# Gate and up in two passes: first units and handover to down reordered, bias table made once per group

## The chip, the cores and the metric

The kernel runs on one core of one Trainium2 chip, as one launch. The metric is the device time of that core in microseconds. Of each kernel the median of several runs is taken; one further execution is recorded by the hardware profiler, and the profile and the trace come from it.

## The reference

x has 1024 rows of 512. It is normalised (layernorm); the result goes through a quantised gated feed-forward block, whose output passes a silu and gates the output of an ALiBi attention with 32 query heads in 8 groups of 4. Weights of the feed-forward block are integers with a zero and a scale per 128 input rows.

```python
def dequantize(w, s, z):                      # groups of 128 rows
    return (w - repeat(z, 128)) * repeat(s, 128)

xn   = (x - mean(x)) / sqrt(var(x) + 1e-5)
gate = silu(xn @ dequantize(gate_w, gate_s, gate_z))     # 512 -> 1792
up   = xn @ dequantize(up_w, up_s, up_z)
ffn  = (gate * up) @ dequantize(down_w, down_s, down_z)  # 1792 -> 512

q, k, v = xn @ Wq.T, xn @ Wk.T, xn @ Wv.T     # 32, 8, 8 heads of 128
q, k    = rmsnorm(q, q_norm_w), rmsnorm(k, k_norm_w)
bias    = where(rel > 0, -1e30, slope[head] * rel)       # rel = key - query
attn    = softmax(q @ k.T / sqrt(128) + bias) @ v        # per head
out     = x + (attn @ Wo.T) * silu(ffn)
```

## The kernel before

**Order.** Every engine's instructions stand in the order in which the program text issues them: the schedule is manual on all five engines, there is no planner. All DMAs are issued on SP's queue. So a line's place in the text decides what it waits behind on its engine. Matmuls of float data run as two or three products of high and low parts; `split_r` (L95) makes such a pair with an ACT copy (L97, the high part) and a DVE subtraction (L99, the low part).

**Layernorm and the first units.** There are 8 row tiles of 128; tiles 0 to 3 are the first half of the columns of xnT, tiles 4 to 7 the second. A tile gets statistics (L281) and moments (L284) on DVE, is normalised (L302 on DVE for the first half, L300 on ACT for the second), transposed by TensorE (L309) and split into xth and xtl. PSUM in this stage is four buffers of two banks each (`pair`, L139), handed out in the order in which they are released.

Gate and up are 14 units of 128 hidden columns. A unit's weights are loaded as integers (`gu_load`, L154), its zeros are spread over the partitions by two matmuls into z_ps (`gu_spread`, L163), and DVE subtracts them (`gu_subtract`, L174, the tile guq). The scales are applied to the four partial sums j = 0 to 3 of the input groups: j even by ACT (L189), j odd by DVE, which adds the scaled sum to the one before (L191); POOL adds the two results (`gu_total`, L195). m = 0 is gate, m = 1 is up. ACT's silu (L199) and DVE's product h (L204) follow one unit later (`gu_finish`, with `behind` holding the unit that is still to be finished). Units 0, 1 and 2 are done twice with half the columns, since the second half of xnT isn't there yet: (0,0), (1,0), (2,0), then (0,1), (1,1), (2,1). Units 3 to 13 take all 1024 columns. The second half's statistics stand inside and after unit (0,0), tiles 4 and 5 are normalised before unit (1,0) and tiles 6 and 7 after it.

**Down.** 14 passes, one for each 128 hidden rows, two column halves each, with twelve 128x512 matmuls to a half (L103 to L105), summed in PSUM over all passes. `dn_load` loads integers, zeros and scales (two passes ahead), `dn_dequant` subtracts on DVE (L389) and multiplies on POOL (L390) one pass ahead, `dn_split_w` and `dn_split_h` make the parts. Pass 0's weights are dequantised before unit 13 and split halfway in it; pass 1's within pass 0. Ahead of down stand also the first value projection's column norms (`norms`, L456 and the seed L82, L83), their application (`scale`, L463) and the norm weights (`norm_weights`, L411 to L417).

**Projections and attention.** Twelve projections (kv, q, q, four times) make q, k and v, which go to scratch memory and back. q's and k's inverse norms are refined on POOL in three newton steps (`newton`, L520 to L523). Attention runs over 8 groups, four blocks of 256 queries and four heads: scores on PE, then DVE adds the bias table `trel` times a scalar and takes the row minimum (L718), ACT takes the exponential (L719) and the high half-precision part (L729), DVE the low part (L738), SP transposes by DMA to pT (L739), PE multiplies with the values and with Wo. The table is made for each head and block by POOL (`relative`, L695), one unit ahead; its width is that of the block.

Of the kernel before, what the change touches and what calls it, by code (L numbers as in the profile page):

```python
# [21 lines left out]
P = 128  # L22
S = 1024
# [39 lines left out]


@with_exitstack
def attention_gated_by_ffn_kernel(ctx, tc, x, gu_w, gu_z, gu_s, dn_w, dn_z, dn_s, wq, wkv, wo, qnw, knw, out):
# [47 lines left out]
    cs = const.tile([P, 1], F32, name="cs")  # L114
# [61 lines left out]
    gu_sums, behind = {}, []  # L176

    def gu_scaled(unit, m, j, ps):
# [3 lines left out]
        if j == 0:  # L182
            two = wp.tile([P, 2, S], F32, tag=("wh", "wl")[m], name=f"g{m}_{it}_{tb}", bufs=2)
            for i in range(2):
                gu_sums[unit, m, 2 * i] = two[:, i, :w]
# [4 lines left out]
        else:  # L190
            ve.scalar_tensor_tensor(a, ps, scale, a, ALU.mult, ALU.add)  # L191

# [13 lines left out]
    def gu_finish(k):  # L206

        if behind:
            (gu_gate, gu_h)[k](behind[0])

    def gu_unit(it, tb, subtract=None, first=False, halfway=lambda: None, late=False):
        unit = (it, tb)
        w = gu_int[it]
        if subtract is not None:
            gu_spread(subtract)
        if not late:
            gu_finish(0)
        for m in range(2):
            ws = slice(m * P, m * P + P)
            banks = {}  # L220
            for j in range(KT):
# [30 lines left out]
                elif j % 2 and not (first and m == 0):  # L252
                    for i in (j - 1, j):
                        gu_scaled(unit, m, i, banks[i])
                elif j == KT - 1:
                    for i in range(KT):
                        gu_scaled(unit, m, i, banks[i])
                if m == 0 and j == 1 and not late:
                    gu_finish(1)
            gu_total(unit, m)  # L260
            if m == 0:
                halfway()
        if late:
            gu_finish(0)
            gu_finish(1)
        behind[:] = [unit]
# [25 lines left out]
    def ln_norm(t):  # L292
        half, r = divmod(t, HT)
        xn[t] = gp.tile([P, DM], F32, tag="hl" if t % 2 else "hh", name=f"xn{t}", bufs=3)
        if half:
            if r == 0:
# [7 lines left out]
    def ln_transpose(t):  # L304
        if t % 2 == 0:
            xt_ps["pair"] = pair(f"xt_ps{t}")
        xt_ps[t] = xt_ps["pair"][:, t % 2, :].rearrange("p (j c) -> p j c", j=KT)
# [34 lines left out]
    gu_load(3)  # L342

    def second_stats(*ts):
        for t in ts:
            ln_stats(t)
        for t in ts:
            ln_moments(t)

    def second_split(*ts):  # L350
        for t in ts:
            ln_transpose(t)
        for t in ts:
            ln_split(t)

    gu_unit(0, 0, 1, True, halfway=lambda: second_stats(4, 5))
    second_stats(6, 7)
    ln_rstd(1)
    ln_norm(4)
    ln_norm(5)  # L360
    gu_unit(1, 0, 2, late=True)
    ln_norm(6)
    ln_norm(7)
    second_split(4, 5)
    gu_unit(2, 0, halfway=lambda: second_split(6, 7))
    gu_unit(0, 1)
    gu_unit(1, 1)
    gu_unit(2, 1, 3)
# [4 lines left out]
    def dn_load(it):  # L373
        if it % 2 == 0:
            wi = gp.tile([P, 2, DM], I32, tag="wi", name=f"dni{it}", bufs=3)
            sp.dma_start(wi, dn_w[it * P : (it + 2) * P, :].rearrange("(t p) c -> p t c", p=P))
            wf = wi.bitcast(F32)
# [571 lines left out]
```

## Time and profile before

| | |
|---|---|
| median of 3 runs | 1113.13 us (1112.53 to 1117.06) |
| the profiled execution | 1118.34 us |
| its span | 1116.6 us |
| mean granted clock of TensorE | 0.989 |
| DVE busy | 877.4 us (79%) |
| ACT busy | 763.5 us (68%) |
| POOL busy | 507.5 us (45%) |
| bias table L695 on POOL | 128 operations, 145.9 us |
| unit 3's first matmul | 54.22 us |
| first down matmul; second pass | 148.32 us; 159.47 us |

Times in the profile are counted from the start of the span. A group of instructions is named by its line, engine, operation, output and inputs; "xcount" is how many there are. A wait is put down to the instruction that released it. The granted clock is the share of full speed at which TensorE may run[...]. PE is TensorE, PEld its weight loads.

### The profile page before, as it was taken

What the parts mean: (1) busy time and instruction counts of PE and PEld (TensorE: products, weight loads), DVE (VectorE), ACT (ScalarE), POOL (GpSimd) and SP (SyncE); (2) the same over time, 40 slices, a digit from 0 to 9 for tenths busy, and PEclk for the clock granted to TensorE, in tenths of its full rate; (3) what the DMA queues carried; (4) which work ended last, traced back from release to release, by engine and by line L of the source; (5) the groups of instructions that cost most, each with busy time, mean ns of one, the idle gap of its engine ahead of it and who ended that gap; (6) DMA issues with size and microseconds to landing.
All of it is one profiled execution on the core that took longest, in us unless ns stands there. A gap on an engine that the chain in (4) does not pass through costs nothing.

```text
span 1116.6 us, 18808 instructions
## 1 busy us (share of the span) xinstructions
PE 1048.9 (94%) x5900; PEld 765.6 (69%) x5900; DVE 877.4 (79%) x1698; ACT 763.5 (68%) x2031; POOL 507.5 (45%) x617
## 2 busy tenths in 40 slices
PE   7899979999999999897899999999999999998996
PEld 5677658878888888675566666666666676665664
DVE  6788984525687677688779898798897988968985
ACT  4766543456657575477779688796896888867872
POOL 1455552215676677562324435245243342424642
PEclk9899999999999999999999999999999999999999
DMA  5133225344998989969999999999999999998994
GB/s 176 45 102 102 76 79 155 88 137 113 223 225 170 248 188 232 253 153 215 221 170 210 177 215 215 185 210 197 197 207 183 193 223 177 195 213 188 230 191 122
DMA packets 461634, 198.13 MB, mean 177 GB/s; under 512 B 395810, under 2 KB 421726, under 8 KB 461534
## 3 DMA queue, kind: packets, MB, share of 16 engines
q1 hardware_dynamic: 461534, 196.93, 81.2%
q8 instruction: 46, 0.75, 0.3%
q14 instruction: 54, 0.44, 0.1%
HBM read 71.03 MB, written 29.36 MB: 90 GB/s over the span
## 4 chain that ended last, share of the span: by engine, by line
PE 55%; DMA 14%; DVE 13%; ACT 9%; issue 6%; POOL 3%; SPq 1%; DVEq 0%; ACTq 0%; POOLq 0%
DMA pT<-p 12%; PE gu_ps L226 5%; PE ps_q L103 4%; PE ps_q L104 4%; PE ps_q L105 4%; PE s L103 3%; PE av L103 3%; PE s L104 3%; PE s L105 3%; PE av L104 3%; PE av L105 3%; ACT p L729 3%; PE op L103 3%; PE op L105 3%; PE op L104 2%
## 5 line engine op out<-in xcount | busy, mean ns | idle before, releaser
L695 POOL TENSOR_SCALAR trel<-nrel,rc 128x1024 f32<-128x1024 f32 (+3 forms) x128 | 145.9, 1140 | 304.8 <-DVE row L718 303.0
L738 DVE SCALAR_TENSOR_TENSOR p<-pf,row,p 128x1024 f16<-128x1024 f32 (+7 forms) x256 | 226.0, 883 | 73.4 <-ACT p L729 71.3
L729 ACT ACTIVATE p<-pf,row 128x1024 f16<-128x1024 f32 (+7 forms) x256 | 197.1, 770 | 71.1 <-DMA pT<-p 67.7
L719 ACT ACTIVATE pf<-pf,row 128x1024 f32<-128x1024 f32 (+7 forms) x256 | 197.2, 770 | 50.7 <-DVE row L718 48.5
L718 DVE CUSTOM_DVE_ANT_0 pf<-s,trel,cs 128x1024 f32<-128x1024 f32 (+7 forms) x256 | 207.0, 809 | 2.5 <-PE s L105 1.3
L103 PE MATMUL av<-pT,vT 128*128 128x256 f16 (+1 forms) x640 | 170.8, 267 | 22.3 <-DMA pT<-p 21.8
L104 PE MATMUL av<-pT,vT 128*128 128x256 f16 (+1 forms) x640 | 168.1, 263 | 0.0
L105 PE MATMUL av<-pT,vT 128*128 128x256 f16 (+1 forms) x640 | 167.9, 263 | 0.0
L103 PE MATMUL s<-kT,qT 128*128 128x512 f16 (+3 forms) x384 | 125.2, 326 | 14.1 <-DVE row L718 13.4
L103 PEld LDWEIGHTS <-vT 128*128 128x128 f16 x640 | 62.3, 97 | 101.3 <-issue 81.1
L104 PE MATMUL s<-kT,qT 128*128 128x512 f16 (+3 forms) x384 | 125.2, 326 | 0.0
L105 PE MATMUL s<-kT,qT 128*128 128x512 f16 (+3 forms) x384 | 123.6, 326 | 0.0
L103 PE MATMUL op<-woh,oh 128*128 128x512 f32 x248 | 121.4, 489 | 0.0
L103 PE MATMUL ps_q<-wh_q,xth 128*128 128x512 f32 x256 | 101.3, 396 | 0.0
L105 PE MATMUL ps_q<-wh_q,xtl 128*128 128x512 f32 x256 | 99.7, 390 | 0.0
L104 PE MATMUL ps_q<-wl_q,xth 128*128 128x512 f32 x256 | 99.6, 389 | 0.0
L105 PE MATMUL op<-woh,ol 128*128 128x512 f32 x248 | 98.1, 396 | 0.0
L104 PE MATMUL op<-wol,oh 128*128 128x512 f32 x248 | 97.7, 394 | 0.3 <-POOL wol L689 0.3
L689 POOL TENSOR_TENSOR wol<-wor,woh 128x512 fp32r<-128x512 f32 x32 | 55.4, 1730 | 46.5 <-ACT woh L688 46.5
L195 POOL TENSOR_TENSOR g_None<-g_None 128x1024 f32<-128x1024 f32 x22 | 54.7, 2486 | 43.1 <-DVE g_None L191 43.0
L104 PEld LDWEIGHTS <-vT 128*128 128x128 f16 x640 | 63.2, 99 | 13.7 <-issue 4.3
L529 POOL TENSOR_TENSOR f_q<-f_q,inv_q 128x512 f32<-128x512 f32 x64 | 71.4, 1134 | 1.4
(155 smaller groups left out, 2427.7 us busy)
## 6 DMA issues: line engine op xcount, KB each, us to landing
qd<-tr_q SPq DMA_DIRECT2D x64, 256.0 KB, 3.4
qT<-qd SPq DMA_DIRECT2D x32, 512.0 KB, 4.2
wq<-in_wq SPq DMA_DIRECT2D x32, 256.0 KB, 3.9
wor<-in_wo SPq DMA_DIRECT2D x32, 256.0 KB, 3.3
gui<-in_gu_w SPq DMA_DIRECT2D x13, 512.0 KB, 3.6
wkv<-in_wkv SPq DMA_DIRECT2D x16, 256.0 KB, 3.9
vd<-v SPq DMA_DIRECT2D x64, 64.0 KB, 2.8
kd<-tr_kv SPq DMA_DIRECT2D x64, 64.0 KB, 1.9
```

The costliest lines, as they stand in the source:

```text
L103: te.matmul(ps, lhsT=lh, rhs=rh, start=first, stop=False)
L104: te.matmul(ps, lhsT=lh, rhs=rl, start=False, stop=False)
L105: te.matmul(ps, lhsT=ll, rhs=rh, start=False, stop=last)
L195: ge.tensor_tensor(a, a, gu_sums.pop((unit, m, 2)), ALU.add)
L226: te.matmul(banks[j][:, k, :], lhsT=w[:, j, ws], rhs=x[:, j, k * 512 : k * 512 + 512], start=x is xth, stop=x is xtl)
L529: ge.tensor_tensor(f, f, ib, ALU.mult)
L689: ge.tensor_tensor(wol[g, i], raw, woh[g, i].bitcast(F32), ALU.subtract)
L695: ge.tensor_scalar(trel[u][:, S - w :], nrel[:, S - w :], rc, float(SLOPES[g * NH + hh]), ALU.mult, ALU.mult)
L718: ve.tensor_tensor_reduce(p, ps, trel[u][:, S - w :], cs, 3e38, ALU.add, ALU.min, least[:, c])
L719: se.activation(p, p, AF.Exp, bias=least[:, c], scale=-1.0, accum_out=total[:, c])
L729: se.activation(p16[u, qt][:, :, 0, :], pf[u, qt], AF.Copy, scale=scale[:, qt : qt + 1])
L738: ve.scalar_tensor_tensor(lo, p, scale, hi, ALU.mult, ALU.subtract)
```

## The change

It has three parts.

1. First units. Each transposed tile gets a PSUM pair of its own. The zero subtraction of units 1 and 2 and the loads of units 3 to 5 stand ahead of unit (0,0). The second half's statistics, moments, inverse deviation and norms all stand after unit (0,0); tiles 6 and 7 are normalised on DVE instead of ACT. All four tiles are transposed and split after unit (1,0). Unit (0,0) is evicted by `gu_first`: ACT scales three of the four sums, and the fourth, on DVE, with two additions on POOL, is held back (`rest`) until the norms have been issued. The silu and the product h of two-pass units stand at the ends of later units.
2. Handover. The value norms of the first projection are made one unit later, their application in down pass 9, the norm weights in pass 5. Pass 0's weights are dequantised in unit 12 and pass 1's in unit 13, with both operations on DVE; pass 0's parts are made in the first quarter of unit 13. Unit 13's totals, silu and h move to passes 1 to 4. In down, loads run three passes ahead, dequantisation two, and both h halves are split one pass ahead.
3. Bias table. One table for each group, for the last of its four slopes, over all 1024 columns. Each head's scalar in L718 is a column of `cs`, which holds the ratio of its slope to the last one's; q is scaled by the inverse ratio in the last newton step, which takes four small operations in place of one.

```diff
+STEEPER = [float(SLOPES[i]) / float(SLOPES[NH - 1]) for i in range(NH)]
...
-    cs = const.tile([P, 1], F32, name="cs")
+    cs = const.tile([P, NH], F32, name="cs")
...
-    gu_sums, behind = {}, []
+    gu_sums, behind = {}, ([], [])
...
-            two = wp.tile([P, 2, S], F32, tag=("wh", "wl")[m], name=f"g{m}_{it}_{tb}", bufs=2)
+            if tb is None or m == 0:
+                tag = m if tb is None else (it + tb + 1) % 2
+                two = gu_sums[unit, "tile"] = wp.tile([P, 2, S], F32, tag=("wh", "wl")[tag], name=f"g{m}_{it}_{tb}", bufs=2)
+            else:
+                two = gu_sums[unit, "tile"][:, :, 512:]
...
+    def gu_first(m, banks):
+
+        two = wp.tile([P, 2, S], F32, tag=("wh", "wl")[m], name=f"g{m}_first", bufs=2)
+        parts = [two[:, 0, :512], two[:, 1, :512], two[:, 0, 512:]]
+        for j, a in enumerate(parts):
+            se.activation(a, banks[j], AF.Copy, scale=gsT[:, 0, m, j : j + 1])
+        gu_sums[(0, 0), m, 0] = parts[0]
+
+        def rest():
+            a, b, c = parts
+            ve.scalar_tensor_tensor(c, banks[3], gsT[:, 0, m, 3:4], c, ALU.mult, ALU.add)
+            ge.tensor_tensor(a, a, b, ALU.add)
+            ge.tensor_tensor(a, a, c, ALU.add)
+
+        return rest
...
-        if behind:
-            (gu_gate, gu_h)[k](behind[0])
-
-    def gu_unit(it, tb, subtract=None, first=False, halfway=lambda: None, late=False):
+        if behind[k]:
+            (gu_gate, gu_h)[k](behind[k].pop(0))
+
+    def gu_unit(it, tb, subtract=None, first=False, halfway=lambda: None, finish=True, meanwhile=lambda: None, total=True):
         unit = (it, tb)
         w = gu_int[it]
+        rest = []
         if subtract is not None:
             gu_spread(subtract)
-        if not late:
+        if finish and tb is None:
...
-                elif j % 2 and not (first and m == 0):
+                elif j % 2 and not first:
                     for i in (j - 1, j):
                         gu_scaled(unit, m, i, banks[i])
-                elif j == KT - 1:
-                    for i in range(KT):
-                        gu_scaled(unit, m, i, banks[i])
-                if m == 0 and j == 1 and not late:
+                if m == 0 and j == 1 and finish and tb is None:
                     gu_finish(1)
-            gu_total(unit, m)
+                    meanwhile()
+            if first:
+                rest.append(gu_first(m, banks))
+            elif total:
+                gu_total(unit, m)
+            for _ in range(finish if tb is not None else 0):
+                gu_finish(m)
             if m == 0:
                 halfway()
-        if late:
-            gu_finish(0)
-            gu_finish(1)
-        behind[:] = [unit]
+        for k in range(2):
+            behind[k].append(unit)
+        return rest
...
-        if half:
-            if r == 0:
+        if t in (HT, HT + 1):
+            if t == HT:
...
-        if t % 2 == 0:
-            xt_ps["pair"] = pair(f"xt_ps{t}")
-        xt_ps[t] = xt_ps["pair"][:, t % 2, :].rearrange("p (j c) -> p j c", j=KT)
+        xt_ps[t] = pair(f"xt_ps{t}")[:, 0, :].rearrange("p (j c) -> p j c", j=KT)
...
-    gu_load(3)
-
-    def second_stats(*ts):
-        for t in ts:
-            ln_stats(t)
-        for t in ts:
-            ln_moments(t)
-
-    def second_split(*ts):
-        for t in ts:
-            ln_transpose(t)
-        for t in ts:
-            ln_split(t)
-
-    gu_unit(0, 0, 1, True, halfway=lambda: second_stats(4, 5))
-    second_stats(6, 7)
+    for it in (1, 2):
+        gu_spread(it)
+        gu_subtract(it)
+    for it in (3, 4, 5):
+        gu_load(it)
+
+    rest = gu_unit(0, 0, first=True, finish=False)
+    for t in range(HT, NT):
+        ln_stats(t)
+        if t > HT:
+            ln_moments(t - 1)
+    ln_moments(NT - 1)
     ln_rstd(1)
-    ln_norm(4)
-    ln_norm(5)
-    gu_unit(1, 0, 2, late=True)
-    ln_norm(6)
-    ln_norm(7)
-    second_split(4, 5)
-    gu_unit(2, 0, halfway=lambda: second_split(6, 7))
-    gu_unit(0, 1)
-    gu_unit(1, 1)
-    gu_unit(2, 1, 3)
+    for t in range(HT, NT):
+        ln_norm(t)
+    for f in rest:
+        f()
+    gu_unit(1, 0, finish=False)
+    for t in range(HT, NT):
+        ln_transpose(t)
+        ln_split(t)
+    gu_unit(2, 0, finish=2)
+    gu_unit(0, 1, finish=1)
+    gu_unit(1, 1, finish=1)
+    gu_unit(2, 1, 3, finish=1)
...
-            wf = wi.bitcast(F32)
-            wh = gp.tile([P, 2, DM], F32R, tag="wq", name=f"dnh{it}", bufs=3)
-            wl = gp.tile([P, 2, DM], F32R, tag="dwl", name=f"dnl{it}")
-            dn_raw["pair"] = (wi, wf, wh, wl)
+            dn_raw["pair"] = (wi, wi.bitcast(F32))
...
-    def dn_dequant(it):
-        wi, wf, wh, wl, zi, si = dn_raw[it]
+    def dn_dequant(it, engine=ge):
+        wi, wf, zi, si = dn_raw[it]
         ve.tensor_tensor(wf, wi, zi, ALU.subtract)
-        ge.tensor_tensor(wf, wf, si, ALU.mult)
+        engine.tensor_tensor(wf, wf, si, ALU.mult)
     def dn_split_w(it):
-        wi, wf, wh, wl, zi, si = dn_raw.pop(it)
-        split_r(wf, wh, wl)
-        dn_w_hl[it] = (wh, wl)
+        if it % 2 == 0:
+            wh = gp.tile([P, 2, DM], F32R, tag="wq", name=f"dnh{it}", bufs=3)
+            wl = gp.tile([P, 2, DM], F32R, tag="dwl", name=f"dnl{it}")
+            dn_w_hl["pair"] = (wh, wl)
+        dn_w_hl[it] = tuple(w[:, it % 2, :] for w in dn_w_hl["pair"])
+        split_r(dn_raw.pop(it)[1], *dn_w_hl[it])
...
-        ve.tensor_scalar(cs, wm, 1.0 / (Q_SCALE * Q_SCALE * math.sqrt(HD)), None, ALU.mult)
-        ve.reciprocal(rc, cs)
+        for i in range(NH):
+            ve.tensor_scalar(cs[:, i : i + 1], wm, STEEPER[i] / (Q_SCALE * Q_SCALE * math.sqrt(HD)), None, ALU.mult)
+        ve.reciprocal(rc, cs[:, NH - 1 : NH])
...
-            c = Q_SCALE if last and self.kind == "q" else 1.0
             ge.tensor_tensor(w, a, y, ALU.mult)
             ge.tensor_tensor(w, w, y, ALU.mult)
-            ge.tensor_scalar(w, w, -0.5 * c, 1.5 * c, ALU.mult, ALU.add)
+            if last and self.kind == "q":
+                for i in range(NH):
+                    c = Q_SCALE / STEEPER[i]
+                    wi = w.rearrange("p (t g) -> p g t", g=NH)[:, i]
+                    ge.tensor_scalar(wi, wi, -0.5 * c, 1.5 * c, ALU.mult, ALU.add)
+            else:
+                ge.tensor_scalar(w, w, -0.5, 1.5, ALU.mult, ALU.add)
...
-    def down_first():
+    def down_begin():
         dn_split_w(0)
         dn_split_h(0, 0)
+        dn_dequant(1, ve)
...
-        elif it == 3 + 2 * KT:
-            norm_weights()
-        if it == NI - 1:
-            dn_dequant(0)
-        gu_unit(it, None, it + 1 if it + 1 < NI else None, halfway=down_first if it == NI - 1 else lambda: None)
-        if NI - 6 <= it < NI - 2:
-            prepare(0, it - NI + 6)
-        if it == NI - 2:
+        last = it == NI - 1
+        gu_unit(
+            it,
+            None,
+            it + 1 if not last else None,
+            meanwhile={NI - 2: lambda: dn_dequant(0, ve), NI - 1: down_begin}.get(it, lambda: None),
+            total=not last,
+        )
+        if it in (NI - 5, NI - 4):
+            prepare(0, it - NI + 5)
+        if it == NI - 3:
             dn_load(0)
             dn_load(1)
+        if last:
+            dn_load(2)
+            dn_split_h(0, 1)
...
-                    dn_load(it + 2)
-                dn_split_h(it, 1)
-                if it == 0:
-                    gu_finish(0)
+                    dn_dequant(it + 2)
+                if it + 3 < NI:
+                    dn_load(it + 3)
                 if it + 1 < NI:
-                    dn_dequant(it + 1)
-            elif it + 1 < NI:
-                if it == 0:
-                    gu_finish(1)
-                dn_split_h(it + 1, 0)
-                dn_split_w(it + 1)
+                    dn_split_w(it + 1)
+            if it + 1 < NI:
+                dn_split_h(it + 1, tb)
...
-            if it >= NI - 4 and tb:
-                prepare(0, 8 - NI + it)
+            if tb:
+                if it in (1, 2):
+                    gu_total((NI - 1, None), it - 1)
+                elif it == 3:
+                    gu_finish(0)
+                elif it == 4:
+                    gu_finish(1)
+                elif it == 5:
+                    norm_weights()
+                elif it == NI - 5:
+                    prepare(0, 3)
+                elif it >= NI - 4:
+                    prepare(0, 8 - NI + it)
...
-    def relative(u):
-        g, qb, hh = units[u]
-        w = QB * (qb + 1)
-        trel[u] = ap1.tile([P, S], F32, tag="trel", name=f"trel{u}")
-        ge.tensor_scalar(trel[u][:, S - w :], nrel[:, S - w :], rc, float(SLOPES[g * NH + hh]), ALU.mult, ALU.mult)
+    def relative(g):
+
+        trel[g] = ap1.tile([P, S], F32, tag="trel", name=f"trel{g}")
+        ge.tensor_scalar(trel[g], nrel, rc, float(SLOPES[g * NH + NH - 1]), ALU.mult, ALU.mult)
...
-        ve.tensor_tensor_reduce(p, ps, trel[u][:, S - w :], cs, 3e38, ALU.add, ALU.min, least[:, c])
+        g, qb, hh = units[u]
+        ve.tensor_tensor_reduce(p, ps, trel[g][:, S - w :], cs[:, hh : hh + 1], 3e38, ALU.add, ALU.min, least[:, c])
...
-            if qt == 0 and u + 1 < len(units):
-                relative(u + 1)
...
+                    relative(g + 1)
```

## The prediction

> **What bounds the kernel now.** The page's first part and its slices come first.
>
> ```profile
> PE 1048.9 (94%) x5900; PEld 765.6 (69%) x5900; DVE 877.4 (79%) x1698; ACT 763.5 (68%) x2031; POOL 507.5 (45%) x617
> ...
> PE   7899979999999999897899999999999999998996
> ```
>
> TensorE is busy for 94% of the span, so a change that leaves its work alone can win at most the 67.7 us (1116.6 - 1048.9) in which it idles, plus the time in which it is busy at half clock. The weak slices are the first two, the sixth (140 to 167 us), and the attention from slice 21 on. Next, the windows by stage; columns are the stretch, its length, busy us of PE, PEld, DVE, ACT, POOL (with counts), granted clock, DMA share and GB/s.
>
> ```profile
> 22.92:26.33 3.41, 1.25 (x6) 0.70 (x4) 2.96 (x11) 1.04 (x3) 1.06 (x1) 1.00 0.00 0
> 26.33:29.75 3.42, 3.10 (x10) 2.49 (x11) 2.40 (x5) 3.38 (x6) 0.64 (x1) 0.50 0.49 153
> 33.16:36.57 3.41, 1.43 (x9) 0.79 (x7) 2.19 (x4) 2.65 (x6) 0.00 (x0) 1.00 0.01 2
> 36.57:43.40 6.83, 6.43 (x15) 4.31 (x15) 4.97 (x8) 3.41 (x7) 2.55 (x2) 0.50 0.00 0
> 159.45:162.87 3.42, 3.40 (x7) 2.43 (x8) 2.49 (x4) 1.01 (x2) 1.45 (x1) 0.50 0.69 197
> 240.00:450.00 210.00, 210.00 (x933) 173.34 (x931) 145.47 (x294) 130.55 (x630) 143.32 (x288) 1.00 0.87 196
> 482.00:1096.00 614.00, 579.15 (x3869) 395.55 (x3869) 527.06 (x1122) 485.75 (x1150) 253.12 (x234) 1.00 0.99 200
> ```
>
> A stretch of 3.41 us in which PE was busy for under half of it (37%, 42%) is followed by one or two at clock 0.50. [...] The projections (240 to 450) keep PE busy without a break; what other engines gain or lose there is hidden. Then the waits:
>
> ```profile
> POOL trel L695 <- DVE row L718: 303.0, 108, 6.5
> ...
> PE av L103 <- DMA pT<-p: 21.8, 18, 3.2
> ...
> PE s L103 <- DVE row L718: 13.4, 19, 1.8
> ```
>
> In attention PE waits for transposed probabilities (21.8 us) and for DVE to free scores (13.4). POOL waits 303 us for DVE before making a bias table, and nothing waits for a table. Last, the timeline at the handover from gate/up to down:
>
> ```profile
> 153.62 2.88 DVE L389 TENSOR_TENSOR dni<-dni,dnz 128x512 f32<-128x512 int32 x1
> ...
> 156.59 2.18 POOL L390 TENSOR_TENSOR dni<-dni,dns 128x512 f32<-128x512 f32 x1 [0.63 <-DVE dni L389]
> ...
> 158.80 0.62 ACT L97 CAST dnh<-dni 128x512 fp32r<-128x512 f32 x1 [7.03 <-POOL dni L390]
> ...
> 159.47 0.79 PE L103 MATMUL dn_ps<-dnh,hh 128*128 128x512 f32 x1 [3.13 <-ACT dnh L97]
> ```
>
> PE's 3.13 us gap is the end of a chain: DVE subtraction (0.68 us when undisturbed, 2.88 here beside POOL's total at 153.25), POOL product, ACT cast.
>
> [...] L389 above, L82 2.34 us at 112.83 beside a POOL total (0.29 for its like, L83)[...]. [...] here the 128x512 product is 1.30 us on POOL at its best, DVE's like 0.68.
>
> **Part A, first units.** Before, PE ends unit (0,0) at about 20.6 us and starts unit 3 at 54.22: 33.6 us for five half-width units of 16 matmuls (0.227 us apart: 3.65 each, 18.2 in all), 16 transposes and a z_ps pair (0.53). PE's losses there: a gap of 2.47 at 26.65 (waits guq, L174), 1.98 at 35.49 (xtl, L99), half clock in three windows (5.1), the rest in waits for banks.
>
> After, guq1 and guq2 are made before unit (0,0) (1.21 each, 15.5 to 17.9, DVE was idle for part of that), so the 2.47 gap goes; PE runs half of unit (1,0), then stalls for banks. What is late next: DVE does statistics, rstd and two norms to about 24.3 (two xn at about 0.5 instead of on ACT), the two deferred sums to 25.75 (2 x 0.75); PE is held from 22.45 to 25.1. Unit (0,0)'s eviction is now six ACT copies (0.68) and two DVE operations instead of four and four; four POOL adds (1.28) replace two, and nobody needs them until the silu much later. The window 26.33 to 29.75 probably stays at half clock. The transposes of tiles 4 to 7 then run 27.6 to 30.4, unit (2,0) to 34.1, and the three second-half units with stalls of 1.0 (ACT's table load 1.28 before the first silu) and 1.1. DVE gives a check: from 24.3 on it has 2 sums 1.5, twenty L191 at 0.68 (13.6), four splits 2.8, five products h 3.5, guq3 1.2: 22.6, ending at 46.9 at the earliest. With some 2.5 us of waits for ACT and PE I take unit 3's first matmul at 49.4 against 54.22: **-4.8 us**. Bounds: -6.0 (waits of 1.3 only) and -1.8 (one more half-clock window, 1.7[...]).
>
> Waits added: in unit (1,0), DVE's sums stand behind statistics of all four tiles; behind them waits the bank that PE needs, counted above. SP's loads of units 3 to 5 are issued earlier and behind no wait that unit 3 needs.
>
> **Part B, handover.** Unit 11 loses norm_weights (L411 to L417, about 2.7 us of DVE from 122.45 to 125.1) and unit 12 the scale (L463, 1.25); the kv norms (0.41 + 2.34 + 0.29 = 3.0) come one unit later. A full unit has 7.54 us of DVE (four L191 at 1.28, h 1.21, guq 1.21) per 8.1 us of PE, so each of these shows as a gap: before, 0.90 at 116.69, 0.65 at 124.78, 0.98 at 134.43. I keep the 0.90 for the norms and put unit 12's start at 128.65 instead of 129.86. From there, before: unit 12, unit 13, first down pass to 159.47, plus 1.7 lost in the half-clock window, effectively 161.2. After: unit 13 starts 8.81 later (0.68 of dequantisation product moved to DVE included), the first down pass 9.84 later, the second 7.55 later, at 154.85. Of these 26.2 us, 20.8 are matmuls (8.1 + 7.6 + 5.1 of the pass whose start overlaps) and 5.4 are stalls, none over 2 us[...]: **-6.3 us**. The 3.13 gap goes because weight 1's chain is done in unit 13: DVE product 0.7 for POOL's 1.3 to 2.2. POOL's totals of unit 13 (2.4 to 2.7 each), silu and h (1.2) move into passes 1 to 4; a pass has 5.44 us of PE against about 2.75 of DVE, which hides them[...]. norm_weights and the scale go into passes 5 and 9 the same way, and weight loads are issued one pass earlier on SP, with their buffers free. Bounds: -7.3 (one us of stalls less) and -3.3 (half-clock window 1.7[...]).
>
> **Part C, bias table and newton.** 128 POOL operations (145.9 us) become 8 of 128x1024 (about 1.66 each, 13.3). None was waited for, so POOL's own saving is worth nothing. [...] L738 takes 21.6 us more than its per-shape minimum in total, 7.1 of it overlapping trel, the rest wol (L689) and others that stay. PE's gaps in attention follow pT transposes in SP's order more than L738, so of 7.1 I take a little: **-0.5**. The last newton step of q has four POOL operations of 128x4 for one of 128x16: 48 more at 0.2 to 0.5 us, 10 to 25 us of POOL, mostly in the stage where POOL is busy 68% and PE 100%: hidden. Ends: -4[...] and +3 (transposes meet loads differently: DMA share 0.99).
>
> **Sum.** -4.8 - 6.3 - 0.5 = -11.6. Against the profiled execution, 1118.34 us (span 1116.6 and 1.7 around it): 1106.7, span 1105. That execution is 5.2 above the median of the runs, 1113.13; the same difference from the median gives **1101.5 us**.
>
> **Rivals.**
> 1. [...] 11.1 + 7.1 = 18.2, 1094.9 us. For: DVE is 86% busy in attention. Against: PE waits mostly for transposes.
> 2. The first units stay DVE-bound and gain nothing; only the handover and C remain: 1113.1 - 6.8 = 1106.3. For: DVE's sum above ends only 7.3 us before 54.22. Against: the removed 2.47 gap.
> 3. The change moves work without shortening the chains: both at their poor ends, attention +3: -1.8 - 3.3 + 3, 1111.0. Against: the 3.13 gap has one chain, and it is cut.
> 4. Slower: the longer newton. If 0.6 us more on POOL per half makes DVE's halves (L541) late, SP blocks behind its transposes, the value stores behind them come late, and PE waits at a kv projection as it does once now, at 453.22 (2.88 and 1.7 of half clock). Five more such stalls: +22.9, less 11.6 from the rest, 1124.4. It decides only once lateness exceeds the PSUM slack of about four tiles (2.8 us each). Against: L541 waited for POOL only 7.8 us in all.
>
> **Chances.** Forecast 0.50; rival 1 0.15; rival 2 0.15; rival 3 0.13; rival 4 0.07. A measurement tells about 0.5% (5.6 us) from no change: below 1107.6 is faster, above 1118.7 slower. Forecast, rival 1 and most of rival 2 (0.12) are faster: 0.77; rival 3 and 0.03 of rival 2 within: 0.16; rival 4 slower: 0.07. The range runs from rival 1 to rival 3, 1095 to 1111.
>
> **What would show it.** A: unit 3's first matmul near 49.4, no gap after guq, at most one half-clock window after 20 us. B: no window at 0.50 near 155, first down matmuls about 3 us after unit 13, second pass starting near 150 (154.85 less A's 4.8). C: trel x8, L738's mean (883 ns) lower by up to 28 ns, PE idle from 482 to 1096 (34.9 us: 614.0 - 579.15) about the same. Wrong if a new half-clock window appears in A or B, if down passes exceed 5.44 us, or if attention's idle moves by over 4.

## The result, and the profile after

The changed kernel takes 1097.68 us (median of 4 runs, 1096.72 to 1098.42) against 1113.59 (4 runs) before. The ratio is 0.9851, with a 95% interval of 0.9828 to 0.9875: 16 us less, where 11.6 were forecast. The profiled execution took 1098.13 us with a span of 1096.4, 20 us below that of before, which lay 5 us above its kernel's median. So stage by stage the profiles tell where time went, and only the medians how much it was in all.

Page of the changed kernel, busy time by engine and PE's slices:

```profile
PE 1043.1 (95%) x5900; PEld 763.1 (70%) x5900; DVE 878.5 (80%) x1703; ACT 761.5 (69%) x2031; POOL 393.3 (36%) x545
...
PE   7999999999999999898899899999999999999997
```

PE has the same 5900 matmuls and is busy for 5.8 us less (1048.9 before): fewer of them ran at half clock (mean granted clock 0.992 for 0.989). The weak sixth slice is gone. POOL has lost 114 us.

The starts of a few matmuls divide the gain. The spreading of zeros, z_ps, of the next unit stands first in a unit. In the profiled executions, in us:

| start of | before | after | gain so far |
|---|---|---|---|
| z_ps at the start of unit 3 | 53.43 | 47.88 | 5.55 |
| z_ps at the start of unit 12 | 129.86 | 122.66 | 7.20 |
| second down pass | 159.47 | 148.01 | 11.46 |
| last down matmul | 231.84 | 219.13 | 12.7 |
| fourth kv projection | 431.14 | 418.43 | 12.7 |
| seventh q projection | 457.55 | 446.96 | 10.6 |
| end of the span | 1116.6 | 1096.4 | 20.2 |

Windows of the first units, columns as in the prediction. They are laid so that the granted clock changes at their edges, 3.41 us apart in this trace:

```profile
20.27:23.68 3.41, 1.34 (x5) 0.80 (x6) 2.97 (x11) 2.38 (x5) 0.16 (x1) 1.00 0.19 79
23.68:27.09 3.41, 3.41 (x10) 2.53 (x10) 2.44 (x4) 1.55 (x4) 3.33 (x3) 0.50 0.02 5
27.09:30.51 3.42, 3.27 (x22) 2.62 (x21) 2.74 (x5) 2.78 (x6) 2.79 (x3) 1.00 0.00 0
...
33.92:37.33 3.41, 2.47 (x11) 1.75 (x10) 2.24 (x4) 1.83 (x5) 1.01 (x2) 1.00 0.00 0
37.33:40.75 3.42, 1.92 (x8) 1.25 (x8) 3.42 (x5) 2.82 (x5) 1.47 (x2) 1.00 0.00 0
```

One window has PE busy for 39% and is followed by one at 0.50; the later ones stay at 72% and 56% and keep the full clock. Before, there were three windows at half clock between 26 and 44 us, and one at 16 to 19.5.

Timeline at the handover, after. The first two lines are the gap at pass 0, the others the one at pass 2:

```profile
144.87 0.68 DVE L101 TENSOR_TENSOR hl<-h,hh 128x512 fp32r<-128x512 f32 x1
...
145.61 0.50 PE L107 MATMUL dn_ps<-dnh,hl 128*128 128x512 f32 x1 [0.87 <-DVE hl L101]
...
150.94 2.86 POOL L217 TENSOR_TENSOR g_None<-g_None 128x1024 f32<-128x1024 f32 x1
151.45 3.49 DVE L101 TENSOR_TENSOR hl<-h,hh 128x512 fp32r<-128x512 f32 x2
...
154.40 0.50 PE L107 MATMUL dn_ps<-dnh,hl 128*128 128x512 f32 x1 [0.33 <-DVE hl L101]
```

The 3.13 us gap is gone, and so is the half-clock window behind it. The slow DVE operations moved with POOL's totals: L101 now takes 3.49 us for two beside the total in pass 1 (two of the same take 1.29 us at 146.67), where there is slack for most of it: pass 2 lasts 6.07 us (153.45 to 159.52) where an undisturbed one lasts 5.44.

Waits of the changed kernel in attention:

```profile
PE av L105 <- DMA pT<-p: 19.9, 17, 3.0
...
PE s L105 <- DVE row L759: 6.6, 9, 1.8
```

The wait for transposes is nearly the same (21.8 before). The wait for DVE to free scores is half of what it was (13.4 before). That is the part of the gain that I had not counted. How much of it is the table's, the experiments show.

### The profile page after: what moved, and what is told of

It reads as the page before. It is cut to its first block, busy times and chain, and to the rows that moved or that the text cites. A ratio compares the mean times of both kernels' runs of the same rounds, so it can differ in the third digit from the quotient of the medians.

```text
span 1096.4 us, 18629 instructions
## 1 busy us (share of the span) xinstructions
PE 1043.1 (95%) x5900; PEld 763.1 (70%) x5900; DVE 878.5 (80%) x1703; ACT 761.5 (69%) x2031; POOL 393.3 (36%) x545
## 4 chain that ended last, share of the span: by engine, by line
PE 61%; DMA 13%; DVE 10%; ACT 8%; issue 5%; POOL 3%; SPq 0%; DVEq 0%; ACTq 0%; POOLq 0%
DMA pT<-p 12%; PE gu_ps L249 6%; PE ps_q L105 4%; PE ps_q L106 4%; PE ps_q L107 4%; PE s L105 4%; PE s L106 3%; PE s L107 3%; PE av L105 3%; PE op L105 3%; PE op L106 3%; PE op L107 3%; PE av L106 3%; PE av L107 3%; ACT p L770 3%
## 5 line engine op out<-in xcount | busy, mean ns | idle before, releaser
L779 DVE SCALAR_TENSOR_TENSOR p<-pf,row,p 128x1024 f16<-128x1024 f32 (+7 forms) x256 | 219.9, 859 | 69.3 <-ACT p L770 67.0
L730 POOL TENSOR_TENSOR wol<-wor,woh 128x512 fp32r<-128x512 f32 x32 | 58.1, 1816 | 427.4 <-ACT woh L729 379.0
L105 PE MATMUL av<-pT,vT 128*128 128x256 f16 (+1 forms) x640 | 170.8, 267 | 20.5 <-DMA pT<-p 19.9
L807 ACT ACTIVATE oh<-av,rv 128x256 fp32r<-128x256 f32 x128 | 58.9, 460 | 23.1 <-PE av L107 22.3
L813 DVE SCALAR_TENSOR_TENSOR ol<-av,rv,oh 128x256 fp32r<-128x256 f32 x128 | 61.2, 478 | 14.2 <-ACT oh L807 14.1
```

What stands on the lines that cost most here:

```text
L105: te.matmul(ps, lhsT=lh, rhs=rh, start=first, stop=False)
L730: ge.tensor_tensor(wol[g, i], raw, woh[g, i].bitcast(F32), ALU.subtract)
L779: ve.scalar_tensor_tensor(lo, p, scale, hi, ALU.mult, ALU.subtract)
L807: se.activation(oh, av_ps[u], AF.Copy, scale=rv[:, g : g + 1])
L813: ve.scalar_tensor_tensor(ol, av_ps.pop(u), rv[:, g : g + 1], oh.bitcast(F32), ALU.mult, ALU.subtract)
```

## The experiments

Twelve runs in three groups of four; the ninth, e9, is the whole change once more. Each group ran on one chip, with the kernel before beside it. A ratio is that to the kernel before on the same chip, and its change in us is worked out from that. "Attention" below is the time from the last q projection matmul to the end of the span.

**The parts alone.**

Each of these applies whole hunks of the change's diff to the kernel before: e1 those of part 1 (the sums, `behind` and `gu_first`, layernorm, the order of the first units), e3 those of part 3 (`STEEPER`, `cs`, `newton`, `relative` and its uses), e4 all but those of part 3. e2 has those of part 2 (the functions of down, the loops over units 3 to 13 and over down) and, in the old `gu_unit`, the two arguments that they use:

```diff
-    def gu_unit(it, tb, subtract=None, first=False, halfway=lambda: None, late=False):
+    def gu_unit(it, tb, subtract=None, first=False, halfway=lambda: None, late=False, meanwhile=lambda: None, total=True):
...
                 if m == 0 and j == 1 and not late:
                     gu_finish(1)
-            gu_total(unit, m)
+                    meanwhile()
+            if total:
+                gu_total(unit, m)
```

First units: 

> The kernel before with part 1 alone (first units). Theory (the gain of the first units is the earlier start of unit 3 and is carried to the end, nothing more): unit 3's z_ps at 47.9 instead of 53.4 us, the handover as before (first to second down pass 11.1 us, the window of half clock after it may or may not stand), about 5.5 us less than before, 0.995. Rival (the gain is only kept together with the handover, because another wait takes it back at unit 11 to 13): second down pass less than 3 us earlier than before, total within 2.5 us of before.

Ratio 0.9966 (0.9952 to 0.998), 3.8 us. In the trace z_ps of unit 3 comes at 47.4 and the last down matmul at 225.6, 6.2 before its place in the kernel before: the theory holds as far as down. The end shows less: 5.5 us lies just outside the interval (2.2 to 5.4). Why isn't shown. The later stages differ from execution to execution by more than I assumed: attention took 604.5 us here and 603.8 in the kernel before, with nothing changed in it, but 600.2 in the next experiment.

Handover: 

> The kernel before with part 2 alone (handover to down). Theory: first to second down pass 6.9 us instead of 11.1 and no window at half clock after it, the last down matmul 7.1 us earlier than before, total about 7.1 less, 0.9936. Rival (part of it came from the shift of the clock's windows by the first units): last down matmul 5.4 or less earlier, with a window at 0.50 after 140 us.

Ratio 0.9932 (0.9917 to 0.9948), 7.6 us. First to second pass took 6.9 us (153.67 - 146.74), no window at half clock followed, and the last down matmul came at 224.8, 7.1 earlier. The places hold to a tenth, the time to half a us.

Table: 

> The kernel before with part 3 alone (bias table once per group, four-piece last step of newton for q). Theory now (the recorded result is 4 us better than my sum, and attention is where the rest lies): 3 to 4 us less than before, 0.997, from fewer waits of PE for DVE to free scores (13.4 us before, 6.6 after) and L738 faster by 6 us in sum. Rival (my recorded estimate: nobody waits for a table, so nothing): 0.5 us or less. Second rival: 0.5 or slower, because the newton pieces cost what the table gives.

Ratio 0.9972 (0.9956 to 0.9988), 3.1 us. My recorded estimate (next to nothing) falls. The waits of this kernel:

```profile
PE s L105 <- DVE row L726: 5.2, 6, 1.8
```

The group of the low parts, with busy time, mean ns and idle time before:

```profile
L746 DVE SCALAR_TENSOR_TENSOR p<-pf,row,p 128x1024 f16<-128x1024 f32 (+7 forms) x256 | 217.6, 850 | 73.2 <-ACT p L737 70.5
```

The same group in the kernel before, where PE waited 13.4 for scores:

```profile
L738 DVE SCALAR_TENSOR_TENSOR p<-pf,row,p 128x1024 f16<-128x1024 f32 (+7 forms) x256 | 226.0, 883 | 73.4 <-ACT p L729 71.3
```

All but the table: 

> Parts 1 and 2 together, the bias table as before. Theory: 12.5 us less than before, 0.9888, and so 3 to 4 us above the whole change; PE's wait for scores about 13 us, L738 in sum about 226 us. Rival (table worth nothing): within 1 us of the whole change, 0.985, and PE's wait for scores falls anyway, as the phase of attention against the DMA queues is another.

Ratio 0.9916 (0.99 to 0.9932): 9.4 us, where I expected 12.5. With the table it is 0.9851, and the intervals don't meet: 7.2 us for the table here, against 3.1 alone. In the trace the first two parts are whole: the last down matmul comes at 219.2, as with the whole change. Where the median loses 3 us of the 12.5 isn't shown. PE's wait for scores was 8.8 us, above the 6.6 with the table but below the 13 expected, so part of the wait also depends on how attention falls against the rest. L738's counterpart took 225.1 us, as expected.

Over all profiles, e5 and e6 left out, the two kinds of kernel stand apart in DVE's low parts and in PE's wait:

| | low parts on DVE, us | PE's wait for scores, us | PE idle in attention, us |
|---|---|---|---|
| table per head (before, e1, e2, e4, e7) | 224.5 to 226.0 | 8.8 to 13.4 | 37.7 to 43.3 |
| table once per group (after, e3, e8 to e12) | 216.4 to 219.9 | 5.2 to 7.6 | 34.6 to 38.3 |

In the mean the wait for scores is 5.0 us shorter with one table (6.5 against 11.5), not the 6.8 of the first pair of profiles.

**What the table's work cost.** POOL's load is put back, once with reads and once without; each run has one of the two marked lines.

```diff
+    def idle_pool(u):
+        g, qb, hh = units[u]
+        for i in range(qb + 1):
+            d = ap1.tile([P, QB], BF16, tag="idle", name=f"idle{u}_{i}", bufs=1)
+            ge.tensor_scalar(d, nrel[:, i * QB : (i + 1) * QB], rc, float(SLOPES[g * NH + hh]), ALU.mult, ALU.mult)   # e5
+            ge.memset(d, 0.0)                                                                                         # e6
...
+            if qt == 0 and u + 1 < len(units):
+                idle_pool(u + 1)
```

> The whole change, and POOL does as much idle work in attention as the tables took: for each head and block one operation per 256 columns that multiplies a piece of nrel into a tile that nobody reads (320 operations, about 0.48 us each, 154 us; the table's were one longer operation each). Nothing waits for them. Theory[...]: L738's sum rises from 219.9 to about 226, PE's waits for DVE to free scores from 6.9 to 10 or more, and 4 to 7 us of the gain are lost: 1102 to 1105, 0.989. Rival (the gain is another phase of attention against the DMA queues, and POOL's work is worth nothing): within 1.5 us of the whole change, 0.985.

Ratio 0.9915 (0.9896 to 0.9934): the whole gain of the table is given back (0.9916 without it), though apart from one wait of 0.7 us nobody waits for this work. PE's wait in this kernel:

```profile
PE s L105 <- DVE row L765: 11.6, 15, 2.4
```

The groups of the low parts and of the idle work:

```profile
L785 DVE SCALAR_TENSOR_TENSOR p<-pf,row,p 128x1024 f16<-128x1024 f32 (+7 forms) x256 | 222.3, 868 | 69.3 <-ACT p L776 67.0
...
L741 POOL TENSOR_SCALAR idle<-nrel,rc 128x256 bf16<-128x256 f32 x316 | 186.1, 589 | 29.0
```

PE's wait for scores is back. The low parts rose to 222.3, less than the 226 expected. POOL's own pieces took 589 ns in the mean for a median of 479.

> As the run before, but POOL's idle operations only write (a memset of 256 columns each, 320 of them) and read nothing from SBUF. Theory[...]: L738's sum stays at 218 to 220, the time within 1.5 us of the whole change, 0.985. Rival (any work of POOL on SBUF blocks DVE): as with the reading operations, 2 us or more lost.

Ratio 0.9885 (0.9867 to 0.9904), 3.8 us above the whole change's 0.9851 where at most 1.5 were expected. By its time this run is on the rival's side, but its attention speaks against the writes as the cause. PE's wait for scores:

```profile
PE s L105 <- DVE row L765: 7.2, 10, 1.8
```

The same two groups:

```profile
L785 DVE SCALAR_TENSOR_TENSOR p<-pf,row,p 128x1024 f16<-128x1024 f32 (+7 forms) x256 | 219.2, 856 | 73.5 <-ACT p L776 70.8
...
L741 POOL MEMSET idle<- 128x256 bf16 x316 | 100.2, 317 | 15.3
```

100 us of writing leave DVE's 219 us and PE's wait as they are with the table. Attention took 598.4 us, between the two profiles of the whole change (595.9 and 598.6). The profiled execution lost time elsewhere: 1.2 us before unit 3, where its clock stood at half from 11.8 to 18.6 us, and 4.9 us instead of 4.1 in a stall of the last kv projection. Whether the other three executions lost theirs there too isn't shown. The timed difference to e5, 0.003, is within what the intervals allow.

The idle work of e5 is also longer in all (186 us for 100), so the sums alone would leave open that any POOL work delays DVE by its length. The single instructions settle it. Among the 256 low-part multiplications of each trace, take those that overlap idle operations and no other work of POOL, and compare each with the mean of its shape beside an idle POOL. In e5 there are 94: 30 took over 40 ns longer, 4.7 us in sum. In e6 there are 50: none did, and their sum is 0.1 us. For 128x512 the means are 740 ns alone, 747 beside memsets and 821 beside reads. So in these two runs the operations that read delayed DVE, and those that only write did not. An operation that computes without reading was not run.

```diff
             ge.tensor_tensor(w, w, y, ALU.mult)
+            if last and self.kind == "q":
+                for i in range(NH):
+                    wi = w.rearrange("p (t g) -> p g t", g=NH)[:, i]
+                    ge.tensor_scalar(wi, wi, -0.5 * c, 1.5 * c, ALU.mult, ALU.add)
+            else:
+                ge.tensor_scalar(w, w, -0.5 * c, 1.5 * c, ALU.mult, ALU.add)
```

> Parts 1 and 2 with the table as before (the run without table), and the last newton step of q in four pieces, with the same factor in each. Theory (the 48 additional POOL operations are hidden in the projections): within 1.5 us of the run without table, 0.9916. Rival (they delay DVE's halves and SP): the stall at the last kv projection grows over 4.1 us or others like it appear, and 3 us or more are lost.

Ratio 0.9913 (0.9893 to 0.9933) against 0.9916 without the pieces. In the timed runs they cost nothing that can be seen. In the changed kernel a piece takes 243 ns in the mean; 48 more of them are 12 us of POOL. The five more stalls of the rival on the slower side of my forecast don't appear. But its sign of one longer stall does: PE waits 5.0 us at the last kv projection in this trace and 3.1 without the pieces. The profiles of the four kernels without pieces (before, e1, e2, e4) have 2.9 to 3.7 us there, those of the nine with them, e8 aside, 3.6 to 5.6. From the fourth kv to the seventh q projection it is 26.4 to 27.5 us against 27.1 to 29.6. By the means that is 1.3 us, which I take as an estimate of what the pieces cost; the medians can't tell it from none.

**A stall that stayed.** In both kernels PE stops once at the last kv projection (2.88 us before, 4.06 after), since ACT waits for a v16 buffer (one of three that hold value tiles until they are stored; 8.3 us after) whose store stands late in SP's queue.

```diff
-        if k == len(projections) - 3:
+        if k == len(projections) - 4:
             load_keys(0)
             load_values(0)
             load_queries(*blocks[0])
+        if k == len(projections) - 3:
             relative(0)
```

> The whole change, and the first keys, values and queries of attention are loaded one projection earlier, in a q projection, so that these three DMAs no longer stand in SP's queue ahead of the value stores of the last kv projection. Theory (the stall of 4.06 us at 441.7 us, and the window of half clock of 6.8 us around it, come from SP's queue: ACT waits 8.3 us for a v16 buffer that a store must release): stall gone or under 1.5 us, no window at 0.50 there, 3 to 6 us less than the whole change, about 1093, 0.981. Rival (SP's queue is full there anyway, weight loads and transposes do it): stall still over 2.5 us, within 1.5 us of the whole change.

Ratio 0.9871 (0.9854 to 0.9888): no faster than the whole change. Waits of this kernel from 425 to 450 us:

```profile
ACT v L521 <- DMA vd<-v: 7.7, 3, 4.5
...
PE ps_q L105 <- DVE v L522: 2.0, 1, 2.0
PE ps_kv L105 <- DVE v L522: 1.7, 2, 1.4
```

The long stall became three short ones (1.36, 0.36 and 1.97 us), and no window at half clock was left there, but the sum is nearly the same (3.7 for 4.1). SP issues a transpose, a weight load, a q store and two value stores for each tile, about 3.8 us (435.35 to 439.13 us in its timeline), where a tile takes PE 2.75. So SP is behind without the three loads too, as the rival says, though no single stall is as long as the 2.5 us that it named. From the fourth kv to the seventh q projection this trace has 26.2 us, the shortest of all twelve; the timed runs show no gain from it, and I would not keep this version. More v16 buffers, which might cover the lag, were not tried.

**Pieces undone.** The whole change was repeated beside three kernels that take one piece back.

> The whole change once more, beside the three runs that undo one piece each, so that they can be compared on one chip. Every theory: 0.985 within its interval; 1.5 us above the recorded 1097.7 would mean that runs of different calls can't be compared closer than that.

Ratio 0.9856 (0.9827 to 0.9886): 0.985 within its interval, as expected. The median, 1099.37, is 1.7 us above the first one, so medians of different groups can't be compared more closely than that; the ratios differ by 0.0005.

```diff
-    for it in (1, 2):
-        gu_spread(it)
-        gu_subtract(it)
-    for it in (3, 4, 5):
-        gu_load(it)
+    gu_load(3)
...
-    rest = gu_unit(0, 0, first=True, finish=False)
+    rest = gu_unit(0, 0, 1, first=True, finish=False)
...
-    gu_unit(1, 0, finish=False)
+    gu_unit(1, 0, 2, finish=False)
```

> The whole change, but units 1 and 2 get their zero subtraction (L176, 1.21 us of DVE each) inside units (0,0) and (1,0) as before, and the loads with it. Theory (the stretch from 24 us to unit 3 is bound by DVE, and the two subtractions were put into time in which DVE was idle): unit 3 starts about 2.4 us later (z_ps at 50.3 instead of 47.9), total 2 to 3 us more. Rival (the gain of the first units is the clock windows that went and the finishes that moved): unit 3 less than 1 us later.

z_ps of unit 3 came at 48.13 against 47.67 in the repeat: 0.46 us, where the theory had 2.4 and the rival less than 1. Counted from the first gate/up matmul, which came 0.5 us earlier here, the stretch is 0.95 us longer. Ratio 0.9879 (0.9857 to 0.9901); the median is 3.0 us above the repeat's, but the intervals overlap, so the time doesn't decide and the trace speaks for the rival. The stretch is not bound by DVE's sum: DVE still waits for ACT between its evictions, and the norms came 0.8 us earlier (20.96 for 21.71 in the whole change) for the subtraction that was left out ahead of them.

```diff
-            meanwhile={NI - 2: lambda: dn_dequant(0, ve), NI - 1: down_begin}.get(it, lambda: None),
+            meanwhile={NI - 2: lambda: dn_dequant(0), NI - 1: down_begin}.get(it, lambda: None),
...
-        dn_dequant(1, ve)
+        dn_dequant(1)
```

> The whole change, but the dequantisation products of down passes 0 and 1 on POOL as before, at their new places. Theory (the earlier place and the totals that no longer stand beside them do it, not the engine): first to second down pass 6.9 to 8.2 us, at most 1.5 us more in all. Rival (POOL's product in the chain is what made the gap): a gap of 2 us or more before the second pass, with a window of half clock, 3 to 5 us more.

First to second pass 6.2 us, and the last down matmul at 217.5, 1.4 us ahead of the repeat (218.9): the products on DVE cost 1.4 us, as much as the two of 0.69 us that DVE no longer does. So what gains is not the engine. Ratio 0.9848 (0.9823 to 0.9873): in the whole the 1.4 us can't be told from none. Of the versions run it is the one I would keep, by its trace.

```diff
-            total=not last,
...
-                if it in (1, 2):
-                    gu_total((NI - 1, None), it - 1)
-                elif it == 3:
-                    gu_finish(0)
-                elif it == 4:
-                    gu_finish(1)
+                if it == 0:
+                    gu_finish(0)
+                    gu_finish(1)
```

> The whole change, but unit 13's totals on POOL stay in unit 13 and its silu and product h in the first down pass, as before. Theory (POOL's totals beside DVE's two-input work make the waits at the handover): L101 or L388 over 2 us at the handover again, first to second down pass 9 us or more, 2 to 5 us more in all. Rival (the dequantisation's earlier place is enough): second pass less than 1 us later.

From unit 12 to the last down matmul 98.2 us against 96.4 in the repeat, 1.8 more; ratio 0.9885 (0.9859 to 0.9912). Timeline of this kernel:

```profile
144.02 5.21 POOL L217 TENSOR_TENSOR g_None<-g_None 128x1024 f32<-128x1024 f32 x2 [5.92 <-DVE g_None L197]
...
146.89 2.89 DVE L407 TENSOR_TENSOR dni<-dni,dnz 128x512 f32<-128x512 int32 x1
```

The subtraction L407 takes 2.89 us again beside POOL's totals (0.69 in the whole change), as the theory says, but by then the second pass's weights are ready: first to second pass is 7.0 us, as in the repeat. It is the third pass that comes late, 7.8 us after the second instead of 5.4. Both theories are half right: the deferred totals are worth 1.8 us of the 5.5 between unit 12 and the end of down by these traces, and the remaining 3.7 belong to the rest of the handover, of which the earlier dequantisation is one piece. The norms, the splits and the loads that were moved with it were not undone one by one. The medians lie 3.1 us apart, with intervals that overlap.

## Why the prediction was right, and where it was off

The forecast was 1101.5 us, the result 1097.7: the direction and both places of the first two parts were right, and one term was much too small.

**Part A, -4.8 forecast, 5.5 to 5.8 measured** (unit 3's first matmul at 48.41 instead of 49.4). The one half-clock window that I kept is there, at 23.7, and the three stalls are as written: 2.07 before unit (1,0)'s second half (2.65 forecast), 0.94 and 1.50 in (0,1) and (1,1) (1.0 and 1.1). What the text under-stressed is where the gain comes from. From the first gate/up matmul to unit 3 PE idles 4.9 us after and 5.9 before, one us less. The time at half clock falls from 13.65 to 3.41 us; the 10.24 us are worth 5.1, half of them, an estimate (in the kernel before down matmuls start 0.43 us apart at half clock and 0.23 at full). The forecast's 1.7 us for one such window, half of 3.41, is an estimate of the same kind. So the gap for guq that went (2.47) was largely replaced by the new stall, and in this account most of the gain is the clock.

The account is not a test, and other profiles speak against taking it as a price. The handover alone (e2) had 3.4 us less at half clock here than the kernel before, yet reached unit 3 only 0.4 us earlier: its PE idled 0.5 us longer. And e6, e8 and e12, with 2.8 to 3.5 us more at half clock than the whole change, took about 0.9 us longer. Why the later windows keep the full clock isn't shown either. The share for which PE is busy doesn't settle it. Half clock followed the windows at 37% and 42% in the kernel before, but also one at 67% (12.68 to 16.09 us); after, 72% and 56% were followed by the full clock, but in e2 54% and 56% were not:

```profile
33.55:36.97 3.42, 1.83 (x7) 1.33 (x8) 2.35 (x5) 2.74 (x5) 0.00 (x0) 1.00 0.01 2
36.97:40.38 3.41, 1.92 (x7) 1.02 (x7) 2.76 (x5) 2.27 (x4) 1.26 (x1) 1.00 0.00 0
40.38:43.79 3.41, 3.41 (x10) 2.66 (x9) 2.42 (x4) 1.42 (x3) 1.48 (x2) 0.50 0.00 0
```

So that part 1 starts unit 3 some 5.5 us earlier is shown, its split into stalls and clock only argued. The check by DVE's sum was a floor only, as the tenth experiment shows.

**Part B, -6.3 forecast, 7.2 measured.** Units 3 to 11 gave 1.65 (1.2 forecast), unit 12 to the end of down 5.5 (5.1). No window at half clock, no stall over 2 us: right, though in the kernel before half clock had also followed a stall of 1.98 us (35.49). The second pass started at 148.01; 150.05 was forecast. One of the signs of being wrong did appear, in small: pass 2 exceeded 5.44 us by 0.63. Of the cause I had one piece wrong: "weight 1's chain is done in unit 13: DVE product 0.7 for POOL's 1.3 to 2.2" counts the engine as a gain, and by the trace of e11 it is a loss of 1.4. The poor ends of parts A and B hold 1.3 us each for DVE work beside POOL's, an estimate that no run tested.

**Part C, -0.5 forecast, 3 to 7 measured.** This is the step that failed: "of 7.1 I take a little". I had 7.1 us of L738 beside table work in hand, above the shortest of each shape, and dropped them with the argument that PE's gaps follow the transposes. Most do, and those stayed (21.8 and 19.9 us). But the third wait that I had shown, PE for scores that DVE frees, hangs on DVE, and it fell by 5 us in the mean. The sign that I gave for being wrong appeared: PE's idle time in attention went from 42.9 to 35.4 us in the two profiles. Alone the table gave 3.1 us, on top of the other parts 7.2; L738's work fell by 6.1 to 9.3 us (226.0 to 219.9, 217.6 and 216.7).

The other half of that step was wrong too: "the rest wol (L689) and others that stay". The multiplications that lie mostly beside wol take 6.6 to 7.5 us more than the shortest of their shape in the five kernels with a table per head, and 1.2 to 3.0 in the seven with one per group. In the mean that is 5.0 us, twice the 2.5 us that DVE gained beside the tables themselves. wol in turn takes 57.4 to 58.5 us in sum with one table and 54.9 to 55.7 with one per head; why isn't shown. Attention took 598.9 us in the mean of the seven profiles with the table made once and nothing added (595.9 to 603.7), 602.4 in that of the five with it made per head (600.1 to 604.5): 3.4 us, with ranges that overlap. So the size lies between 3 and 7 and is no closer known. Rival 1, with all 7.1 us on the path, was thus nearer to the result than its chance of 0.15 said. That the table's work delayed DVE was assumed in the forecast. That it was POOL's reads, and not POOL's mere activity, is shown by the single instructions of e5 (30 of 94 over 40 ns longer) and e6 (none of 50); that the delay costs the kernel its gain, by the time of e5 (0.9915 for 0.9916 without the table).

**The sum.** By the traces the first two parts gave 12.7 us, 1.6 more than forecast, and the last kv projection took 2.1 back: from the fourth kv to the seventh q projection 28.5 us against 26.4. About 1.3 of that is what the newton pieces seem to cost, which the forecast had as hidden; the rest is within the scatter of that stage (26.2 to 29.6 us in the twelve experiments). The rival of a slower kernel needed such a stall six times; it comes once. Attention gave 8.0 between these two profiles and the end of the projections 1.7, part of which is that the profiled execution of the kernel before lay 5 us above its median. All three terms were too small, the table's by the most (2.5 to 6.5 us), and a loss that the forecast left out took some of it back: that the sum came within 4 us is in part luck.

## What to carry to other kernels

Work that nobody waits for can still cost: here the table's 120 POOL operations less were worth 3 to 7 us, and DVE's low parts took 6.1 to 9.3 us less without them. Before discounting such work, sum the pace-setter's instruction times over the shortest of their shape, see how much of that lies beside the other engine's operations, and look which wait hangs on the pace-setter (here PE's for scores, 6.5 us for 11.5 in the mean). Where PE idles in short pieces, look at the clock granted in the windows around each: here 4.9 us of stalls went with 3.4 us at half clock and 5.9 us with 13.7, though no run tests where the stalls lie by itself. Move dependent preparation a stage earlier rather than to a faster engine, if that engine is the busier one: here a product took 0.69 us on DVE and 1.30 on POOL at its best, and with two of them on POOL (e11) the last down matmul came 1.4 us earlier.

## What the runs showed of the hardware

- Beside POOL operations that only write, none of 50 low-part multiplications on DVE took over 40 ns longer (e6); beside ones that read, 30 of 94 did (e5), and POOL's own pieces took 589 ns in the mean for 479 at the median.
- L82, a DVE operation that reads one tile, `al`, took 2.34 us beside a POOL total at 112.83 us, and 0.29 at each of its three later places in the kernel before. Why isn't shown. L718, which adds scores from PSUM to the table, was not slowed: 877 ns beside table work and 875 without, for 128x640 in the kernel before.
- The clock's windows did not fall at the same place in each execution: in two executions of the whole change the window at half clock behind unit (0,0) began at 23.68 and at 23.13 us. In e6, e8 and e12 the record shows half clock for 6.8 us from 11 to 12 us on, and unit 3's z_ps came at 49.1 to 49.2; in the other profiles with part 1 it came at 47.3 to 48.1. Their code differs nowhere before 60 us from that of the whole change or of e5, so over 1 us between executions goes with these windows. The place of the window alone doesn't decide it: e1's window began at 11.19, between those of e8 (11.00) and e12 (11.32), and was at half clock for 3.4 us only.
